# The last batch's feed-forward in layer 3: written out for two tiles in turn, over three engines

## The chip, the cores and the metric

The kernel runs on one core of one Trainium2 chip. The metric is the device time of one execution in microseconds (us). One further execution is recorded by the hardware profiler; its trace gives every instruction's start and duration, counted from the first instruction.

## What is computed

Four layers run one after the other on four batches of 256 tokens of 256 numbers. Each layer adds a cross-attention and a feed-forward to its input, each behind a layer norm. The change lies in the very last piece, layer 3's feed-forward, of which this is the core:

```python
def _quant_weight(w):
    scale = jnp.mean(jnp.abs(w)) + EPS
    wq = jnp.clip(jnp.round(w / scale), -1.0, 1.0)
    return (wq, scale)

def _quant_act(x):
    s = jnp.max(jnp.abs(x), axis=-1, keepdims=True) / 127.0 + EPS
    xq = jnp.clip(jnp.round(x / s), -128.0, 127.0)
    return (xq, s)

def _qlinear(x, w):
    wq, ws = _quant_weight(w)
    xq, xs = _quant_act(x)
    y = jnp.einsum('bsi,oi->bso', xq, wq)
    return y * xs * ws
gate = jax.nn.silu(_qlinear(x, w_gate))
up = _qlinear(x, w_up)
return _qlinear(gate * up, w_down)
```

Rows go in with 256 numbers, gate and up have 1024 columns, and down brings them back to 256. A row is rounded to whole numbers by its own largest magnitude, once ahead of gate and up and once more ahead of down.

## The kernel before

Tokens stand on the 128 partitions, so one batch is two tiles, q = 0 and 1. In layer 3 the attention of a batch is a long chain of score and value matmuls (`scores` and `values`), and the feed-forward of the batch before is put between them step by step: `ffn` is a Python generator, and each `yield` in it is a place where other work is written in between. For the last batch no attention is left. The end of `l3` (lines 2052 to 2066) closes the last head with `close`, forms the layer norm with `norms` and `normed`, and then steps the two generators of the two tiles in turn until both are done:

```python
            tail = [ffn(B - 1, q, xn, wide) for q in range(2)]
            while tail:
                tail = [t for t in tail if next(t, self) is not self]
```

Each engine carries out its instructions in the order in which they stand in its own queue, and waits at semaphores for the others. So this loop also sets the order in every queue: tile 0's step, tile 1's step, tile 0's next step. TensorE for instance gets gate of tile 0, gate of tile 1, up of tile 0, up of tile 1, for each half of 512 columns.

The steps of `ffn`, with their lines: `scale_of` takes the row maximum, the scale and its reciprocal (1859, 1860, 1862). Rounding is done by adding and subtracting a large constant RND: one operation scales and adds it (1869), the next subtracts it and clips above (1870), the third clips below and writes bf16 (1872). Two small products make the output scales `sg` (1874, 1875). The tile is transposed on TensorE (1879) and copied out of PSUM (1881). For each half of the 1024 columns follow two gate matmuls, silu as tanh on ScalarE (1890) with (1 + tanh) * gate on VectorE (1891), two up matmuls and the product of both (1896). Then the maximum over all 1024 columns (1859), the rounding in three operations of 1024 columns on VectorE (1900, 1902, 1904), eight transposes (1908), one copy (1910), eight down matmuls, the residual (1917) and the store by SP's DMA queue (1918). All elementwise work is VectorE's but the tanh. `close` ends a head: two transposes (1960), a division (1963, 1965) and two adds to the residual on GpSimd (1970). The statistics of the layer norm are at 1761 and 1762, the normalisation at 1767, the square root for it at 81. Matmuls are all issued by the helper `mm`, line 77. PSUM tiles of the tail come from the pool `ps_s`, three buffers of two banks each.

Of the kernel before, what the change touches and what calls it, by code (L numbers as in the profile page):

```python
# [11 lines left out]
F32 = mybir.dt.float32  # L12
BF16 = mybir.dt.bfloat16
# [4 lines left out]
AF = mybir.ActivationFunctionType  # L18
ALU = mybir.AluOpType
AX = mybir.AxisListType  # L20
# [3 lines left out]
P = 128  # L24
B = 4
S = 256
NT = B * S
D = 256
# [6 lines left out]
RND = 12582912.0  # L35
# [19 lines left out]
I3 = 1024  # L55
# [3 lines left out]
class Kernel:  # L59
# [1669 lines left out]
    def l3(self, first):  # L1729
# [9 lines left out]
        nc, tc, i = self.nc, self.tc, self.i  # L1739
        pairs = [tuple(range(m, min(m + 2, NM))) for m in range(0, NM, 2)]  # L1740
        with ExitStack() as es:
            one = es.enter_context(tc.tile_pool(name="a3one", bufs=1, reuse_waits="tile"))
            two = es.enter_context(tc.tile_pool(name="a3", bufs=2, reuse_waits="tile"))
            self.late3 = es.enter_context(tc.tile_pool(name="a3late", bufs=1, reuse_waits="tile"))
            ps_s = es.enter_context(tc.tile_pool(name="a3s", bufs=3, space=PSUM))
            ps = es.enter_context(tc.tile_pool(name="a3p", bufs=1, space=PSUM))
            ps_o = es.enter_context(tc.tile_pool(name="a3o", bufs=1, space=PSUM))
            mk, idb = self.mk3, self.idb
            self.va3.append(self.values3(self.late3))
            wq, ws = {}, {}  # L1750

            def bank():
                return ps.tile([P, 512], F32, name="b3", tag="tp")

            mv = one.tile([P, B, 2, 2], F32, name="mv3")
            rs = one.tile([P, B, 2], F32, name="rs3")

            def stats(b):
                for q in range(2):
                    t = self.small.tile([P, 6], F32, name="st3")  # L1760
                    nc.vector.bn_stats(t, self.x[b][:, q, :])
                    nc.vector.bn_aggr(mv[:, b, q, :], t)

            def normed(b, r):
                xn = self.xn.tile([P, 2, D], F32, name="xn3", tag="xn")
                for q in range(2):
                    nc.vector.tensor_scalar(
                        xn[:, q, :], self.x[b][:, q, :], mv[:, b, q, 0:1], r[:, q : q + 1], ALU.subtract, ALU.mult
                    )
                return xn  # L1770

            def norms(bs):

                for b in bs:
                    stats(b)
                v = slice(bs[0], bs[-1] + 1)
                self.rstd(rs[:, v, :], mv[:, v, :, 1], 1.0, self.eps5)
# [78 lines left out]
            def scale_of(v, name):  # L1856

                s = self.small.tile([P, 1], F32, name=name + "s")
                nc.vector.tensor_reduce(s, v, AX.X, ALU.max, apply_absolute_value=True)
                nc.vector.tensor_scalar(s, s, 1.0 / 127.0, 1e-5, ALU.mult, ALU.add)  # L1860
                r = self.small.tile([P, 1], F32, name=name + "r")
                nc.vector.reciprocal(r, s)
                return s, r

            def ffn(b, q, xn, take):

                v = xn[:, q, :]
                xs, r = scale_of(v, "xq3")
                nc.vector.tensor_scalar(v, v, r, RND, ALU.mult, ALU.add)
                nc.vector.tensor_scalar(v, v, RND, 127.0, ALU.subtract, ALU.min)  # L1870
                vb = two.tile([P, D], BF16, name="xb3")
                nc.vector.tensor_scalar(vb, v, -128.0, None, ALU.max)
                sg = self.small.tile([P, 3], F32, name="sg3")
                nc.vector.tensor_scalar(sg[:, 0:1], xs, ws["l3_wg"], 0.5, ALU.mult, ALU.mult)
                nc.vector.tensor_scalar(sg[:, 1:2], xs, ws["l3_wu"], sg[:, 0:1], ALU.mult, ALU.mult)
                yield
                tp = take(BF16)[:, : 2 * P].rearrange("p (k t) -> p k t", k=2)
                for k in range(2):
                    nc.tensor.transpose(tp[:, k, :], vb[:, k * P : (k + 1) * P], idb)
                xT = two.tile([P, 2, P], BF16, name="xqT3")  # L1880
                nc.vector.tensor_copy(xT, tp)
                yield
                g = two.tile([P, I3], F32, name="g3")
                for c in range(0, I3, 512):

                    pg = take(F32)
                    for k in range(2):
                        self.mm(pg, xT[:, k, :], wq["l3_wg"][:, k, c : c + 512], k == 0, k == 1)
                    gc = g[:, c : c + 512]
                    nc.scalar.activation(gc, pg, AF.Tanh, scale=sg[:, 0:1])  # L1890
                    nc.vector.scalar_tensor_tensor(gc, gc, 1.0, pg, ALU.add, ALU.mult)
                    yield
                    pu = take(F32)
                    for k in range(2):
                        self.mm(pu, xT[:, k, :], wq["l3_wu"][:, k, c : c + 512], k == 0, k == 1)
                    nc.vector.scalar_tensor_tensor(gc, pu, sg[:, 1:2], gc, ALU.mult, ALU.mult)
                    yield
                hs, r = scale_of(g, "hq3")
                yield
                nc.vector.tensor_scalar(g, g, r, RND, ALU.mult, ALU.add)  # L1900
                yield
                nc.vector.tensor_scalar(g, g, RND, 127.0, ALU.subtract, ALU.min)
                hb = two.tile([P, I3], BF16, name="hb3")
                nc.vector.tensor_scalar(hb, g, -128.0, None, ALU.max)
                yield
                tp = take(BF16).rearrange("p (k t) -> p k t", t=P)
                for k in range(I3 // P):
                    nc.tensor.transpose(tp[:, k, :], hb[:, k * P : (k + 1) * P], idb)
                hT = two.tile([P, I3 // P, P], BF16, name="hT3")
                nc.vector.tensor_copy(hT, tp)  # L1910
                yield
                o = take(F32)[:, :D]
                for k in range(I3 // P):
                    self.mm(o, hT[:, k, :], wq["l3_wd"][:, k, :], k == 0, k == I3 // P - 1)
                nc.vector.tensor_tensor(sg[:, 2:3], hs, ws["l3_wd"], ALU.mult)
                y = two.tile([P, D], F32, name="y3")
                nc.vector.scalar_tensor_tensor(y, o, sg[:, 2:3], self.x[b][:, q, :], ALU.mult, ALU.add)
                nc.sync.dma_start(self.out[b, q * P : (q + 1) * P, :], y)
# [35 lines left out]
                            m == 0, m == NM - 1,  # L1954
                        )

            def close(b, os, h, u):
                tp = bank().rearrange("p (q k) -> p q k", k=P)[:, :2, :]
                for q in range(2):
                    nc.tensor.transpose(tp[:, q, :], os[:, q * P : (q + 1) * P], self.ident)  # L1960
                tv = tp.rearrange("p q (r e) -> p q r e", e=32)
                rc = self.small.tile([P, 2, 4], F32, name="r3")
                nc.vector.reciprocal(rc, tv[:, :, :, HD3])
                t = two.tile([P, 2, 4, HD3], F32, name="t3")
                nc.vector.tensor_tensor(  # L1965
                    t, tv[:, :, :, :HD3], rc[:, :, :, None].to_broadcast([P, 2, 4, HD3]), ALU.mult
                )
                for q in range(2):
                    xt = self.x[b][:, q, h * P : (h + 1) * P].rearrange("p (r u d) -> p r u d", r=4, d=HD3)[:, :, u, :]
                    nc.gpsimd.tensor_tensor(xt, xt, t[:, q], ALU.add)  # L1970

            def beside(b, st):

# [50 lines left out]
            last = done = None  # L2024
            for b in range(B):
# [3 lines left out]
                for n, (h, u) in enumerate(heads):  # L2029
                    o = ps_o.tile([P, S], F32, name="o3")  # L2030
                    for c, ms in enumerate(pairs):
# [6 lines left out]
                        elif last is not None and last[5][-1] == NM - 1:  # L2038
                            os = two.tile([P, S], F32, name="os3")
# [5 lines left out]
                        last = (e, o, st["va"], h, u, ms, b)  # L2045
# [6 lines left out]
            values(*last[:6])  # L2052
            os = two.tile([P, S], F32, name="os3")
            nc.vector.tensor_copy(os, last[1])
            close(last[6], os, last[3], last[4])

            def wide(dt):
                return ps_s.tile([P, 1024 if dt is F32 else 2048], dt, name="w3", tag="s3")[
                    :, : 512 if dt is F32 else 1024
                ]  # L2060

            norms([B - 1])
            xn = normed(B - 1, rs[:, B - 1, :])
            tail = [ffn(B - 1, q, xn, wide) for q in range(2)]
            while tail:
                tail = [t for t in tail if next(t, self) is not self]

    def run(self):
        tc = self.tc
# [157 lines left out]
```

## Time and profile before

| | us |
|---|---|
| median of 8 runs | 2569.15 (2564.02 to 2572.76) |
| the profiled execution's own time | 2570.58 |
| its span, first to last instruction | 2568.8 |
| last attention matmul ends | 2540.25 |
| last VectorE instruction (residual of tile 1) ends | 2565.95 |
| TensorE busy in the whole span | 2435.7 (95%) |
| VectorE, ScalarE, GpSimd busy in the whole span | 1407.7, 1311.1, 841.6 |

In the profile PE is TensorE, DVE VectorE, ACT ScalarE, POOL GpSimd and SP the engine that issues DMAs. A row of a timeline gives start, duration, engine, line, operation, output and inputs, sizes and count; in square brackets stands how long the engine had been idle, and what ended that. Instructions of one line that follow each other are put into one row. A row of a group gives the total busy time and the mean duration in ns behind the bar. The granted clock is the share of its full clock that TensorE was allowed.

### The profile page before, as it was taken

The numbers are of one execution on the slowest core, as the hardware profiler recorded it, in microseconds if no ns is written. First come the engines' busy times: TensorE is split into PE (matmuls) and PEld (weight loads), VectorE is DVE, ScalarE is ACT, GpSimd is POOL, SyncE is SP. The second block draws the span as 40 slices with busy tenths as digits, with TensorE's granted clock in tenths as the row PEclk, the third lists the DMA queues.
The fourth block names the chain that finished last, engine by engine and source line by source line (L and its number), as shares of the span: only waits on it lengthen the run. The fifth ranks groups of instructions, "written<-read, shape, count | busy, mean of one in ns | idle before, by whom it ended". The sixth has DMA issues, their size and how long they took to land.

```text
span 2568.8 us, 47102 instructions
## 1 busy us (share of the span) xinstructions
PE 2435.7 (95%) x17623; PEld 1510.3 (59%) x17623; DVE 1407.7 (55%) x2915; ACT 1311.1 (51%) x3000; POOL 841.6 (33%) x1516
## 2 busy tenths in 40 slices
PE   8989987899989999999999999998999999999997
PEld 5778876777645555555555555565554544544553
DVE  5453534843567777777777777763324324334323
ACT  3234444533654545554545454423336766757875
POOL 1015645223345555555555555541011001011000
PEclk9999998989999999999999999998999999999998
DMA  7165675624601111111111111004310100000000
GB/s 251 49 212 156 175 148 156 215 88 138 224 19 48 47 48 48 47 47 48 47 48 48 47 48 47 9 1 176 125 56 28 34 2 28 6 1 2 6 6 5
DMA packets 96474, 188.45 MB, mean 73 GB/s; under 512 B 15401, under 2 KB 64297, under 8 KB 95050
## 3 DMA queue, kind: packets, MB, share of 16 engines
q1 hardware_dynamic: 80102, 146.50, 17.1%
q0 software_dynamic: 10416, 28.46, 4.8%
q10 hardware_dynamic: 5732, 10.49, 1.3%
q8 instruction: 143, 2.34, 0.4%
q14 instruction: 81, 0.66, 0.1%
HBM read 137.29 MB, written 48.11 MB: 72 GB/s over the span
## 4 chain that ended last, share of the span: by engine, by line
PE 84%; DVE 5%; ACT 3%; issue 3%; DMA 2%; POOL 1%; another core or an unknown queue 0%; ACTq 0%; PEld 0%; SPq 0%; POOLq 0%; DVEq 0%; PEldq 0%
PE s L77 25%; PE o L77 24%; PE fill L1241 3%; PE f2gu L77 3%; PE b L77 3%; PE f1gu L77 2%; PE acc L77 2%; PE tpq L77 2%; PE f0gu L77 2%; PE tpkv L77 2%; PE av L77 2%; PE f0y L77 2%; PE filly L1241 2%; PE f2y L77 1%; PE s L254 1%
## 5 line engine op out<-in xcount | busy, mean ns | idle before, releaser
L1487 ACT ACTIVATE p<-s,nmsm 128x448 f32<-128x448 f32 (+1 forms) x512 | 326.5, 644 | 381.2 <-PE s L77 247.2
L1943 ACT ACTIVATE e<-s 128x1024 f32<-128x1024 f32 (+1 forms) x448 | 404.3, 960 | 159.4 <-PE s L77 154.4
L77 PE MATMUL o<-pT,va 128*128 128x256 f32 (+2 forms) x1920 | 434.2, 379 | 9.5 <-DVE pT L1528 8.0
L77 PE MATMUL s<-kT,qT 128*32 128x448 f32 (+1 forms) x4096 | 427.4, 558 | 11.6 <-ACT kT L1459 8.2
L77 PEld LDWEIGHTS o<-pT,va 128*128 128x128 f32 (+1 forms) x1920 | 347.5, 192 | 130.5 <-issue 89.6
L1522 POOL TENSOR_SCALAR p<-p,rm 128x448 f32<-128x448 f32 (+1 forms) x512 | 324.5, 655 | 6.2
L1483 DVE TENSOR_REDUCE nmsm<-s 128x2 f32<-128x896 f32 (+1 forms) x256 | 287.5, 1124 | 7.9
L77 PE MATMUL s<-qb,kT 32*128 32x256 f32 (+1 forms) x3328 | 268.0, 405 | 11.0 <-ACT e L1943 11.0
L1528 DVE STREAM_TRANSPOSE pT<-p 128x896 f32<-128x896 f32 (+1 forms) x256 | 270.7, 1111 | 9.5 <-POOL p L1522 8.8
L77 PEld LDWEIGHTS s<-kT,qT 128*32 128x32 f32 x4096 | 120.2, 110 | 264.0 <-issue 239.0
L77 PE MATMUL o<-e,va 128*32 128x256 f32 (+1 forms) x3328 | 236.3, 392 | 1.2 <-DVE os L2040 1.2
L77 PEld LDWEIGHTS s<-qb,kT 32*128 32x128 f32 (+1 forms) x3328 | 163.3, 181 | 105.2 <-issue 75.5
L1515 POOL TENSOR_TENSOR rm<-em,tot 32x8 f32<-32x8 f32 x256 | 54.6, 213 | 400.0 <-DVE tot L1512 388.8
L1241 PE MATMUL fill<-wkc_early,ctxT 128*128 128x256 f32 (+1 forms) x572 | 148.7, 412 | 13.9 <-ACT kT_early L1277 12.1
L1970 POOL TENSOR_TENSOR x<-x,t 128x32 f32<-128x32 f32 x64 | 14.7, 252 | 439.6 <-DVE t L1965 439.6
L77 PEld LDWEIGHTS o<-e,va 128*32 128x32 f32 (+1 forms) x3328 | 90.6, 110 | 115.1 <-issue 74.9
L1480 DVE TENSOR_TENSOR s<-s,mask 128x128 f32<-128x128 f32 (+1 forms) x256 | 84.3, 330 | 104.6 <-PE s L77 92.4
L1241 PEld LDWEIGHTS fill<-wkc_early,ctxT 128*128 128x128 f32 (+1 forms) x572 | 114.9, 205 | 36.9 <-ACT kT_early L1277 14.5
L458 POOL DMA_INDIRECT f0xr<-f0xd,f0src x95 | 90.9, 957 | 69.5 <-PE f0y L77 24.4
L1487 ACT ACTIVATION_READ_ACCUMULATOR p<-s,nmsm 128x1 f32 x512 | 101.3, 198 | 0.0
L77 PE MATMUL f2gu<-f2wgu,f2xsT 128*128 x176 | 85.6, 611 | 0.6 <-ACT f2xsT L74 0.3
L566 POOL DMA_INDIRECT f0yt<-f0yd,f0slot x64 | 63.1, 986 | 60.2 <-DVE x L558 29.0
(488 smaller groups left out, 3510.6 us busy)
## 6 DMA issues: line engine op xcount, KB each, us to landing
ctxT<-in_ctxT SPq DMA_DIRECT2D x9, 1664.0 KB
vd<-va_early SPq DMA_DIRECT2D x96, 128.0 KB
kd<-kT_early SPq DMA_DIRECT2D x48, 256.0 KB
kT<-kd SPq DMA_DIRECT2D x16, 768.0 KB
va<-vd SPq DMA_DIRECT2D x16, 768.0 KB
f0yd<-f0ys SPq DMA_DIRECT2D x95, 128.0 KB
wq<-in_l_wq SPq DMA_DIRECT2D x16, 512.0 KB
wo<-in_l_wo SPq DMA_DIRECT2D x16, 512.0 KB
```

The costliest lines, as they stand in the source:

```text
L77: self.nc.tensor.matmul(out, lhsT, rhs, start=start, stop=stop, **kw)
L254: ins = nc.tensor.matmul(s[:, c0:c1], xT[:, k, q * P : (q + 1) * P], ctxT[b][:, k, c0:c1], start=k == 0, stop=k == 1)
L458: nc.gpsimd.indirect_dma_start(out=t, out_offset=None, in_=xd[:, :], in_offset=bass.IndirectOffsetOnAxis(ap=src[:, n : n + 1], axis=0),)
L566: nc.gpsimd.indirect_dma_start(out=yt, out_offset=None, in_=yd[:, :], in_offset=bass.IndirectOffsetOnAxis(ap=slot[:, t, r : r + 1], axis=0),)
L1241: ins = nc.tensor.matmul(tp[:rows, t, :], ctxT[u // NKV2][:, k, c0 : c0 + rows], w[u % NKV2][:, k, :], start=k == 0, stop=k == 1,)
L1480: nc.vector.tensor_tensor(sv, sv, mask[:, 2 * c : 2 * c + 2, : nt - CT, :].rearrange("p n t i -> p n (t i)"), ALU.add)
L1483: nc.vector.tensor_reduce(ms[:, 0, 2 * c : 2 * c + 2], s[:, :, : nt * 32], AX.X, ALU.max, negate=True)
L1487: nc.scalar.activation(p[:, n, : nt * 32], s[:, n, : nt * 32], AF.Exp, bias=ms[:, 0, e : e + 1], accum_out=ms[:, 1, e : e + 1],)
L1515: nc.gpsimd.tensor_tensor(r[32 * a : 32 * a + 32], e[:, a], tot, ALU.mult)
L1522: nc.gpsimd.tensor_scalar(p[:, n, : nt * 32], p[:, n, : nt * 32], r[:, e : e + 1], 1.0, ALU.mult, ALU.mult)
L1528: self.pin(nc.vector.transpose(pT[:, 2 * c : 2 * c + 2, :nt, :].rearrange("p n t i -> p n (t i)"), p[:, :, : nt * 32]))
L1943: nc.scalar.activation(e[:kr, :, :n, :], s[t][:kr, :, :n, :], AF.Exp, scale=1.0 / math.sqrt(HD3))
```

## The change

The last batch gets a method of its own, `last_tokens`, in place of the two generators. In the normalisation and the three roundings ahead of gate and up, tile 0 is VectorE's and tile 1 GpSimd's. The two tiles' first part is written first; then a loop does all the rest of tile 0 and then all the rest of tile 1. Gate and up of one half go to one PSUM tile of two banks. Silu is one ScalarE function that also scales, with its table loaded by an instruction of its own behind the square root. The row maximum is taken by halves into `mx` and then over those two. The first rounding operation ahead of down is a ScalarE activation (scale and RND as bias); the two clips stay with VectorE and go by halves, as do the transposes and copies, one copy on ScalarE and one on VectorE. The output scales are products on GpSimd. The second tile's store is issued by ScalarE. `close` gets a parameter, so that the last head's two adds run on VectorE.

```diff
-            def close(b, os, h, u):
+            def close(b, os, h, u, eng=nc.gpsimd):
...
-                    nc.gpsimd.tensor_tensor(xt, xt, t[:, q], ALU.add)
+                    eng.tensor_tensor(xt, xt, t[:, q], ALU.add)
...
-            close(last[6], os, last[3], last[4])
-
-            def wide(dt):
-                return ps_s.tile([P, 1024 if dt is F32 else 2048], dt, name="w3", tag="s3")[
-                    :, : 512 if dt is F32 else 1024
-                ]
-
-            norms([B - 1])
-            xn = normed(B - 1, rs[:, B - 1, :])
-            tail = [ffn(B - 1, q, xn, wide) for q in range(2)]
-            while tail:
-                tail = [t for t in tail if next(t, self) is not self]
+            close(last[6], os, last[3], last[4], nc.vector)
+
+            self.last_tokens(one, two, ps_s, mv, rs, stats, scale_of, wq, ws)
+
+    def last_tokens(self, one, two, ps_s, mv, rs, stats, scale_of, wq, ws):
...
+        nc, b, idb = self.nc, B - 1, self.idb
+        wide = lambda dt: ps_s.tile([P, 1024 if dt is F32 else 2048], dt, name="w3", tag="s3")
+        eng = (nc.vector, nc.gpsimd)
+        rnd = self.small.tile([P, 1], F32, name="rnd3")
+        nc.gpsimd.memset(rnd, RND)
+        stats(b)
+        self.rstd(rs[:, b, :], mv[:, b, :, 1], 1.0, self.eps5)
+
+        self.pin(nc.scalar.activation(self.small.tile([P, 1], F32, name="one3"), self.eps6, AF.Silu))
+        xn = self.xn.tile([P, 2, D], F32, name="xn3", tag="xn")
+        xT, sg = [], []
+        for q in range(2):
+            v = xn[:, q, :]
+            eng[q].tensor_scalar(
+                v, self.x[b][:, q, :], mv[:, b, q, 0:1], rs[:, b, q : q + 1], ALU.subtract, ALU.mult
+            )
+            xs, r = scale_of(v, "xq3")
+            eng[q].tensor_scalar(v, v, r, RND, ALU.mult, ALU.add)
+            eng[q].tensor_scalar(v, v, RND, 127.0, ALU.subtract, ALU.min)
+            vb = two.tile([P, D], BF16, name="xb3")
+            eng[q].tensor_scalar(vb, v, -128.0, None, ALU.max)
+            t = self.small.tile([P, 3], F32, name="sg3")
+            nc.gpsimd.tensor_tensor(t[:, 0:1], xs, ws["l3_wg"], ALU.mult)
+            nc.gpsimd.tensor_tensor(t[:, 1:2], xs, ws["l3_wu"], ALU.mult)
+            sg.append(t)
+            tp = wide(BF16)[:, : 2 * P].rearrange("p (k t) -> p k t", k=2)
+            for k in range(2):
+                nc.tensor.transpose(tp[:, k, :], vb[:, k * P : (k + 1) * P], idb)
+            t = two.tile([P, 2, P], BF16, name="xqT3")
+            nc.vector.tensor_copy(t, tp)
+            xT.append(t)
+        for q in range(2):
+            gq = two.tile([P, I3], F32, name="g3")
+            mx = self.small.tile([P, 2], F32, name="mx3")
+            for n, c in enumerate(range(0, I3, 512)):
+                w = wide(F32)
+                pg, pu = w[:, :512], w[:, 512:]
+                for t, name in ((pg, "l3_wg"), (pu, "l3_wu")):
+                    for k in range(2):
+                        self.mm(t, xT[q][:, k, :], wq[name][:, k, c : c + 512], k == 0, k == 1)
+                gc = gq[:, c : c + 512]
+                nc.scalar.activation(gc, pg, AF.Silu, scale=sg[q][:, 0:1])
+                nc.vector.scalar_tensor_tensor(gc, pu, sg[q][:, 1:2], gc, ALU.mult, ALU.mult)
+                nc.vector.tensor_reduce(mx[:, n : n + 1], gc, AX.X, ALU.max, apply_absolute_value=True)
+            s, r = scale_of(mx, "hq3")
+            hT = two.tile([P, I3 // P, P], BF16, name="hT3")
+            hb = two.tile([P, I3], BF16, name="hb3")
+            nc.gpsimd.tensor_tensor(sg[q][:, 2:3], s, ws["l3_wd"], ALU.mult)
+            for n, c in enumerate(range(0, I3, 512)):
+                gc, hc = gq[:, c : c + 512], hb[:, c : c + 512]
+                nc.scalar.activation(gc, gc, AF.Identity, bias=rnd, scale=r)
+                nc.vector.tensor_scalar(gc, gc, RND, 127.0, ALU.subtract, ALU.min)
+                nc.vector.tensor_scalar(hc, gc, -128.0, None, ALU.max)
+                tp = wide(BF16)[:, :512].rearrange("p (k t) -> p k t", t=P)
+                for k in range(4):
+                    nc.tensor.transpose(tp[:, k, :], hc[:, k * P : (k + 1) * P], idb)
+                (nc.vector.tensor_copy if n else nc.scalar.copy)(hT[:, 4 * n : 4 * n + 4, :], tp)
+            o = wide(F32)[:, :D]
+            for k in range(I3 // P):
+                self.mm(o, hT[:, k, :], wq["l3_wd"][:, k, :], k == 0, k == I3 // P - 1)
+            y = two.tile([P, D], F32, name="y3")
+            nc.vector.scalar_tensor_tensor(y, o, sg[q][:, 2:3], self.x[b][:, q, :], ALU.mult, ALU.add)
+            (nc.scalar if q else nc.sync).dma_start(self.out[b, q * P : (q + 1) * P, :], y)
```

## The prediction

> **What bounds the kernel now.** I read the page's first and fourth parts, then the timeline of the last 30 us by engine, then the granted clock by stage, and last the rows of operations that the change puts on another engine. The chain's shares by engine:
>
> ```profile
> PE 84%; DVE 5%; ACT 3%; issue 3%; DMA 2%; POOL 1%; another core or an unknown queue 0%; ACTq 0%; PEld 0%; SPq 0%; POOLq 0%; DVEq 0%; PEldq 0%
> ```
>
> TensorE bounds the kernel nearly everywhere, but not where the change lies. The last attention matmul ends at 2540.25 us; what follows is the last batch's feed-forward, 28.5 us up to 2568.8, and nothing of the next stage runs beside it. VectorE in that stretch (start, duration, operation, count):
>
> ```profile
> 2541.57 0.23 DVE L1965 TENSOR_TENSOR t<-b,r 128x64 f32<-128x64 f32 x1
> ...
> 2543.70 0.73 DVE L1767 TENSOR_SCALAR xn<-x,mv,rs 128x256 f32<-128x256 f32 x2
> 2544.35 0.74 DVE L1859 TENSOR_REDUCE xq3s<-xn 128x1 f32<-128x256 f32 x2
> ...
> 2547.26 0.29 DVE L1872 TENSOR_SCALAR xb<-xn 128x256 bf16<-128x256 f32 x1
> ...
> 2553.82 1.40 DVE L1896 SCALAR_TENSOR_TENSOR g<-w,sg,g 128x512 f32<-128x512 f32 x2
> 2555.14 2.33 DVE L1859 TENSOR_REDUCE hq3s<-g 128x1 f32<-128x1024 f32 x2
> ...
> 2557.78 1.40 DVE L1900 TENSOR_SCALAR g<-g,hq3r 128x1024 f32<-128x1024 f32 x2
> 2559.11 1.29 DVE L1902 TENSOR_SCALAR g<-g 128x1024 f32<-128x1024 f32 x2
> ...
> 2565.47 0.48 DVE L1917 SCALAR_TENSOR_TENSOR y<-w,sg,x 128x256 f32<-128x256 f32 x1 [0.39 <-PE w L77]
> ```
>
> The "x2" rows are the point: both tiles pass VectorE in turn, and it has no gap from 2550.47 to 2561.6. TensorE:
>
> ```profile
> 2547.61 0.40 PE L1879 MATMUL w<-idb,xb 128*128 128x128 bf16 x2 [0.65 <-DVE xb L1872]
> 2547.79 1.91 PE L77 MATMUL w<-l_wgb,xqT 128*128 128x512 bf16 x4
> 2549.50 1.56 PE L77 MATMUL w<-l_wub,xqT 128*128 128x512 bf16 x4
> 2561.05 1.89 PE L1908 MATMUL w<-idb,hb 128*128 128x128 bf16 x16 [7.16 <-DVE hb L1904]
> 2562.87 2.56 PE L77 MATMUL w<-l_wdb,hT 128*128 128x256 bf16 x16
> ```
>
> It idles 7 us in the middle. So VectorE bounds this stretch, with two tiles filling each other's waits. The granted clock in it (third figure from the right, after the five engines' busy times):
>
> ```profile
> 2543.90:2550.50 6.60, 3.29 (x11) 1.33 (x12) 4.66 (x22) 2.66 (x3) 0.00 (x0) 0.50 0.00 1
> 2550.60:2557.30 6.70, 2.83 (x10) 0.77 (x8) 6.62 (x9) 1.35 (x2) 0.00 (x0) 1.00 0.00 0
> 2557.50:2564.10 6.60, 3.05 (x22) 2.51 (x23) 5.55 (x14) 0.00 (x0) 0.00 (x0) 0.50 0.00 0
> ```
>
> After idling TensorE runs at 0.50; a 512-column matmul then takes 0.43 (eight from 2547.79 to 2551.21) instead of 0.3 (the four from 2551.21 in 1.25).
>
> **What decides: the order.** The changed program as built has, on TensorE: transposes of tile 0, transposes of tile 1, then gate, up, transposes and down of tile 0, and only then gate and up of tile 1. VectorE has the same order. So nothing of tile 1 past its transposes overlaps tile 0. The change takes VectorE's load away (four (1+tanh)*gate products of 0.69, two scalings of 0.70, half of the first roundings, four small scales), but it gives up the filling of one tile's waits by the other. I therefore add up a serial chain, twice.
>
> **Head.** The two residual adds move from GpSimd (0.25 each, first done at 2542.1, statistics from 2542.16) to VectorE; VectorE's nearest row is the 0.23 product of twice the size, and both adds now stand before the statistics: 0, within 0.1. Normalising tile 1 and its three roundings go to GpSimd, which shows no 128x256 of that operation. These are its bounds (ns of one behind the bar):
>
> ```profile
> L1522 POOL TENSOR_SCALAR p<-p,rm 128x448 f32<-128x448 f32 x256 | 160.0, 642 | 6.2
> L1515 POOL TENSOR_TENSOR rm<-em,tot 32x8 f32<-32x8 f32 x256 | 54.6, 213 | 400.0 <-DVE tot L1512 388.8
> L386 POOL TENSOR_SCALAR f0start<-tok 128x1 f32<-128x1 f32 x1 | 0.2, 243 | 0.0
> ```
>
> A straight line between 243 ns (1 column) and 642 (448) gives 0.47 for 256. VectorE saves one of its 0.37 normalisations, so tile 1's scale comes at about 2544.95 instead of 2545.27. In GpSimd's queue four one-column products stand ahead of the roundings: 4 x 0.21 = 0.84, to 2545.8; then 3 x 0.47 = 1.41, to 2547.2, against 2547.55 now. That is the lower end. The upper end comes from what VectorE's same instruction does beside GpSimd (minimum, median, maximum):
>
> ```profile
> L1767 DVE TENSOR_SCALAR xn<-x,mv,rs x12: 397/409/1335, 1925.4 to 2544.0; 128x256 f32<-128x256 f32 x12
> L1767 DVE TENSOR_SCALAR xn<-x,mv,ss x4: 694/1373/2050, 2153.2 to 2317.9; 128x256 f32<-128x256 f32 x4
> ```
>
> The second group runs while GpSimd normalises keys (2151.55 to 2158.32): it waits for whole GpSimd instructions. If every pair excludes the other, tile 1's first normalisation waits 0.37, and VectorE's three roundings of tile 0 (0.35 + 0.28 + 0.28) stand between GpSimd's: +1.28, to 2548.5. I take 2547.8, nearer the middle since the small products read little. [...] TensorE queues tile 0's gate behind tile 1's transposes, so everything waits for this. First gate matmul 0.24 later (as now, 2547.55 to 2547.79): **2548.05**, between 2547.45 and 2548.75; now 2547.79.
>
> **One tile, from its first gate matmul.** ScalarE's silu waits for gate and up of its half (the wait names the last up matmul): 4 x 0.43 + 0.24 until ScalarE begins (2548.65 to 2548.89 now) = 1.95. Silu 0.69 as the tanh: 2.64. Product with up 0.75 and a gap of 0.03: 3.42. Maximum of a half, 0.69 (the 128x512 row of L1724), to 4.14. The second product waits for that or for the second silu, 4.06 to 4.38, then 0.75 + 0.04 + 0.68: 5.6. Maximum of two, scale 0.15, reciprocal 0.16, gaps: 6.2. Rounding on ScalarE: 512 columns, 0.67 (0.65 for a square, 0.69 for a tanh): 6.9. Two clips of 512 columns on VectorE, 0.42 each (between 0.28 for 256 and 0.69 for 1024): 7.8. Four transposes at 0.107 + 0.22 (now 16 in 1.89): 8.45. ScalarE's copy of 512 columns 0.58: 9.1. Eight matmuls of 256 columns at 0.213: **10.8**, and 11.0 for y. The second half is ready by 9.6, when the first four matmuls still run. At the full clock this is 0.5 (four at 0.3), 0.2 (eight transposes took 0.62 at 2406.93) and 0.65 less (eight such matmuls took 1.05 at 2408.34): 9.45 and 9.65.
>
> **Sum.** Tile 0 at the low clock: 2548.05 + 10.8 = 2558.85 for tile 1's gate. Tile 1 between 9.65 and 11.0; I take 10.5, nearer the low clock, since TensorE again idles about 5 us in each tile: y starts at 2569.35, against 2565.47. That is **+3.9 us**; the end behind it stays (0.48 and 2.85 to the end of the span; the store now goes out by ScalarE's queue, where an issue takes 0.375 against 0.332, both rows of this trace). [...] The profiled execution took 2570.58, 1.4 above the median, so I put +3.85 on the median 2569.15: 2573.0.
>
> **Edits at no cost.** Silu's table load (1.28) follows the square root at 2543.5 and ends by 2544.8, five us before silu; today's tanh load ends at 2546.8, two us before its use, so nothing is gained either. If that cover went, 1.28 would show. The constant's memset (0.09) stands before GpSimd's mask conversion, which idles 66 us for a DMA. Both weight scales are done by 2545.8, needed at 2550; the third one (0.21) has 4 us. SP's queue only loses a store.
>
> **Rivals.** First, on the other side: GpSimd's chain ahead of tile 1's transposes is so slow that the kernel is slower beyond 0.2% (5.1 us, about what a measurement of this kernel can tell from no change). It decides from xb of tile 1 at 2549.05 on. For: the 1.3 to 2.05 us that VectorE's operation took beside GpSimd. Against: those GpSimd instructions were four times larger. With 0.9 instead of 0.47 for its four: +1.7, 2574.7. Chance 0.14. [...] Chance 0.18. Third: the change does overlap the tiles as its words say. VectorE then has 2 x 5.9 us (two products, two maxima, 0.44 small, four clips, copy, y) from 2550.7 on, and some 1 us of matmuls behind the last: y at 2563.5, -2, 2567. The built order speaks against it: 0.06, half of it beyond 0.2%. My forecast, +2.5 to +5.1, has 0.62. Range: +1.7 (all low ends) to +5.1 (2548.75 + 10.8 + 11.0 = 2570.55, all high ends), and up to +6.35 for the first rival; below, 0.85 us for the spread of the runs shown: 2570 to 2575.5. Slower 0.16 (the first rival and a rest of the forecast), faster 0.03, the same 0.81.
>
> **What would show it.** Right: tile 1's gate begins after tile 0's last down matmul, about 11 us after tile 0's; tile 1's xb on GpSimd ends between 2547.2 and 2548.5 on this clock; VectorE has gaps of us where it now has none; the granted clock is 0.50 in much of both tiles. Wrong: tile 1's matmuls between tile 0's, a tile under 9.5 us, GpSimd's 128x256 over 0.9, or a difference before 2541.5.

## The result and the profile after

The changed kernel takes 2577.08 us (median of 12 runs, 2572.39 to 2581.32), the kernel before beside it 2569.48 (34 runs). The ratio is 1.0030, 95% interval 1.0023 to 1.0038: some 7.7 us slower, where 3.85 were forecast and 2575.5 was the upper end of the range. The profiled execution took 2575.34, its span is 2573.6. Up to the last attention matmul both programs are the same, and in this execution the last head ends 3.6 us earlier than in that of before. All times below are therefore counted from one event, **the start of the copy of the last head's sums out of PSUM** (L2054; at 2540.30 before, 2536.71 after), and "the tail" is the stretch from there to the end of the span: 28.55 us before, 36.92 after, **+8.37**. Its three parts:

| us | before | after | difference | predicted |
|---|---|---|---|---|
| head: to the first gate matmul | 7.49 | 9.29 | +1.80 | +0.26 |
| tiles: from there to the start of the last residual (y) | 17.68 | 22.68 | +5.00 | +3.6 |
| end: from there to the end of the span | 3.38 | 4.95 | +1.57 | 0 |

The page's chain of waits moves by a hundredth (TensorE from 84% to 85%) and does not name the cause.

TensorE's timeline of the tail has the tiles one behind the other:

```profile
2545.81 0.39 PE L2090 MATMUL w<-idb,xb 128*128 128x128 bf16 x2 [1.98 <-POOL xb L2083]
2546.00 1.06 PE L77 MATMUL w<-l_wgb,xqT 128*128 128x512 bf16 x2
...
2554.25 0.61 PE L2118 MATMUL w<-idb,hb 128*128 128x128 bf16 x4 [4.63 <-DVE hb L2115]
...
2555.53 1.89 PE L77 MATMUL w<-l_wdb,hT 128*128 128x256 bf16 x8
2557.22 1.06 PE L77 MATMUL w<-l_wgb,xqT 128*128 128x512 bf16 x2
...
2566.70 1.89 PE L77 MATMUL w<-l_wdb,hT 128*128 128x256 bf16 x8
```

The first row waits for GpSimd's xb, and tile 0's gate stands right behind it. Tile 1's gate follows tile 0's last down matmul, 11.22 us after tile 0's. VectorE, which before ran from 2550.47 to 2561.6 without a gap, now waits by turns for ScalarE and TensorE:

```profile
2548.80 0.75 DVE L2105 SCALAR_TENSOR_TENSOR g<-w,sg,g 128x512 f32<-128x512 f32 x1 [2.26 <-ACT g L2104]
...
2553.30 0.43 DVE L2114 TENSOR_SCALAR g<-g 128x512 f32<-128x512 f32 x1 [0.88 <-ACT g L2113]
...
2557.52 0.48 DVE L2124 SCALAR_TENSOR_TENSOR y<-w,sg,x 128x256 f32<-128x256 f32 x1 [1.40 <-PE w L77]
...
2568.68 0.48 DVE L2124 SCALAR_TENSOR_TENSOR y<-w,sg,x 128x256 f32<-128x256 f32 x1 [1.40 <-PE w L77]
```

GpSimd's timeline shows the size that the head turned on (duration is the second figure), and a last small product at 2563.47:

```profile
2540.22 1.39 POOL L2076 TENSOR_SCALAR xn<-x,mv,rs 128x256 f32<-128x256 f32 x1 [13.64 <-DVE rs L82]
...
2543.07 0.58 POOL L2080 TENSOR_SCALAR xn<-xn,xq3r 128x256 f32<-128x256 f32 x1
2543.73 1.07 POOL L2081 TENSOR_SCALAR xn<-xn 128x256 f32<-128x256 f32 x1
2544.90 0.86 POOL L2083 TENSOR_SCALAR xb<-xn 128x256 bf16<-128x256 f32 x1
...
2563.47 0.19 POOL L2110 TENSOR_TENSOR sg<-hq3s,l_wds 128x1 f32<-128x1 f32 x1 [10.97 <-DVE hq3s L1860]
```

Four operations of one size took 1.39, 0.58, 1.07 and 0.86, where the forecast had 0.47 for each.

The granted clock in stretches of the tail (the third figure from the right; the figure behind the window's length is TensorE's busy time):

```profile
2546.20:2549.60 3.40, 3.40 (x9) 0.91 (x6) 1.06 (x3) 0.69 (x1) 0.00 (x0) 0.50 0.00 0
2550.40:2553.70 3.30, 0.00 (x0) 0.00 (x0) 2.28 (x6) 1.24 (x2) 0.19 (x1) 1.00 0.00 0
2553.90:2560.50 6.60, 6.06 (x24) 2.93 (x24) 2.51 (x6) 1.35 (x3) 0.00 (x0) 0.50 0.06 20
2560.70:2563.90 3.20, 0.08 (x1) 0.00 (x0) 2.60 (x6) 0.97 (x2) 0.19 (x1) 1.00 0.00 0
2564.10:2568.70 4.60, 2.99 (x16) 1.72 (x16) 2.06 (x6) 1.62 (x3) 0.00 (x0) 0.50 0.00 0
```

In the two tiles TensorE had the full clock only where it did almost nothing (1.00 with 0.00 and 0.08 us of work), and half of it (0.50) in nearly all its work. Last, the end of the program: the instructions of its closing line, L2223 before and L2282 after (engine's queue, operation, count: minimum, median and maximum in ns, first and last start). Before:

```profile
L2223 POOLq EVENT_SEMAPHORE  x4: 17/17/17, 2568.1 to 2568.7; - x4
L2223 POOLq DRAIN  x3: 45/107/9652, 2541.8 to 2568.6; - x3
L2223 SPq DRAIN  x3: 7/7/7, 2568.0 to 2568.3; - x3
```

After:

```profile
L2282 POOLq EVENT_SEMAPHORE  x4: 17/17/17, 2572.9 to 2573.5; - x4
L2282 POOLq DRAIN  x3: 45/107/9383, 2563.4 to 2573.4; - x3
L2282 SPq DRAIN  x3: 7/7/7, 2571.2 to 2573.1; - x3
```

GpSimd closes with a drain that lasts over 9 us in both. Before, GpSimd's last operation ended at 2542.33, its drain at 2551.49, in the shade of the feed-forward; the end came with SP's drain at 2568.0, when the last store had landed. After, the last operation ended at 2563.66 and the drain only at 2572.81, while SP's drain is done at 2571.3: GpSimd's semaphore event at 2572.9 opens the end.

So there were three theories for the parts, with rivals. **Head:** GpSimd's price, by the kind of operation or by VectorE's work beside it. **Tiles:** the serial order, at a low clock. **End:** GpSimd's closing drain behind the third scale product; the rival was that the last store is late because ScalarE issues it.

### The profile page after: what moved, and what is told of

Same layout as the page of the kernel before. It is cut to its first block, busy times and chain, and to the rows that moved or that the text cites. A ratio compares the mean times of both kernels' runs of the same rounds, so it can differ in the third digit from the quotient of the medians.

```text
span 2573.6 us, 47114 instructions
## 1 busy us (share of the span) xinstructions
PE 2437.2 (95%) x17623; PEld 1509.7 (59%) x17623; DVE 1402.5 (54%) x2909; ACT 1317.1 (51%) x3007; POOL 846.1 (33%) x1525
## 4 chain that ended last, share of the span: by engine, by line
PE 85%; DVE 5%; ACT 3%; DMA 2%; issue 2%; POOL 2%; another core or an unknown queue 1%; SPq 0%; ACTq 0%; PEld 0%; DVEq 0%; PEldq 0%; POOLq 0%
PE s L77 25%; PE o L77 24%; PE fill L1241 4%; PE f2gu L77 3%; PE b L77 3%; PE f1gu L77 2%; PE acc L77 2%; PE tpq L77 2%; PE f0gu L77 2%; PE filly L1241 2%; PE tpkv L77 2%; PE av L77 2%; DMA f0xr<-f0xd,f0src 2%; PE f2y L77 1%; PE f0y L77 1%
## 5 line engine op out<-in xcount | busy, mean ns | idle before, releaser
L1522 POOL TENSOR_SCALAR p<-p,rm 128x448 f32<-128x448 f32 (+1 forms) x512 | 324.4, 655 | 6.2
```

The source lines that it names most:

```text
L1522: nc.gpsimd.tensor_scalar(p[:, n, : nt * 32], p[:, n, : nt * 32], r[:, e : e + 1], 1.0, ALU.mult, ALU.mult)
```

## The experiments

Three chips served. The first four kernels ran beside a kernel before of 2568.8 us, experiments 5 to 8 on a chip where it takes 2526.5, and 9 and 10 on one where it takes 2525.8; so a time is compared only with its own neighbour. Tails are compared across: experiment 7, which leaves the tail as it is, has 28.55 us on its chip like the kernel before. Each time stands with the kernel before that shared its chip.

**1. The third scale product on VectorE.** Changed kernel, with

```diff
-            nc.gpsimd.tensor_tensor(sg[q][:, 2:3], s, ws["l3_wd"], ALU.mult)
+            nc.vector.tensor_tensor(sg[q][:, 2:3], s, ws["l3_wd"], ALU.mult)
```

> The tail is counted from the copy of the last head's sums out of PSUM (L2054) to the end of the span: 28.55 us in the kernel before, 36.92 in the changed one. Theory (a late GpSimd instruction keeps GpSimd's closing drain running after the last store): with the third scale on VectorE the last GpSimd work is tile 1's rounding, the barrier no longer waits for GpSimd, and 1.5 to 1.6 us go from behind the last y; tail 35.4. Rival (the store through ScalarE's queue costs it): nothing goes, 36.9.

Measured: 2574.70 against 2568.76, ratio 1.0026 (1.0014 to 1.0037); tail 35.33, which is 1.59 less, while y starts at 31.91 against 31.97. Its closing line:

```profile
L2282 POOLq EVENT_SEMAPHORE  x4: 17/17/17, 2570.2 to 2570.9; - x4
L2282 POOLq DRAIN  x3: 45/107/10058, 2543.8 to 2570.7; - x3
L2282 SPq DRAIN  x3: 7/7/7, 2570.1 to 2570.4; - x3
```

The drain now begins at 2543.8, GpSimd's event comes right behind SP's drain as it did before. From the start of y to the end it is 3.42 us, against 4.95 in the changed kernel and 3.38 before: the 1.57 of the end is GpSimd's, and the store, still issued by ScalarE here, has at most the 0.04 that is left.

**2. The second store issued by SP.** Changed kernel, with

```diff
-            (nc.scalar if q else nc.sync).dma_start(self.out[b, q * P : (q + 1) * P, :], y)
+            nc.sync.dma_start(self.out[b, q * P : (q + 1) * P, :], y)
```

> Only the last store moves back to SP's queue; the third scale stays on GpSimd. Theory (GpSimd's closing drain): tail unchanged, 36.9, within 0.2. Rival (the store through ScalarE's queue costs it): 35.4.

Measured: 2577.79, ratio 1.0032 (1.0021 to 1.0044); tail 36.91 against 36.92. The rival for the end falls: in the changed kernel it makes no difference which engine issues the store, since GpSimd's drain ends later (2579.0 in this run, where SP's first begins at 2577.4). What the store costs without that drain, experiment 1 shows.

**3. Tile 1's normalisation and roundings on VectorE.** Changed kernel, with

```diff
-        eng = (nc.vector, nc.gpsimd)
+        eng = (nc.vector, nc.vector)
```

> Normalisation and three roundings of tile 1 return to VectorE; all else as in the changed kernel. Theory (GpSimd's four 128x256 operations set the head, since tile 0's gate stands behind tile 1's transposes): the first gate matmul begins 7.0 to 7.4 us after L2054 instead of 9.3, and the whole 2 us are passed on: tail 34.9. Rival (the serial order of the tiles and the low clock are all of it, the head is covered): tail 36.5 or more.

Measured: 2574.86, ratio 1.0023 (1.0011 to 1.0035); tail 34.37, the first gate matmul at 7.10 instead of 9.29. TensorE's timeline:

```profile
2543.65 0.61 PE L2090 MATMUL w<-idb,xb 128*128 128x128 bf16 x4 [5.40 <-DVE xb L2083]
2544.43 1.04 PE L77 MATMUL w<-l_wgb,xqT 128*128 128x512 bf16 x2 [0.17 <-DVE xqT L2092]
```

One engine doing both tiles is 2.2 us earlier than two engines sharing them, and even 0.4 earlier than the kernel before. The tail gained 0.36 us more than the head: tile 1's last two up matmuls took 0.59 instead of 1.00, as at the granted clock of 1.00 in experiment 10.

**4. One late GpSimd instruction in the kernel before.** Two copies of a single column, one behind each tile's y; the rest is untouched and nothing reads them:

```diff
                     nc.vector.scalar_tensor_tensor(y, o, sg[:, 2:3], x, ALU.mult, ALU.add)
+                    if b == B - 1:
+                        nc.gpsimd.tensor_copy(self.small.tile([P, 1], F32, name="late"), y[:, 0:1])
```

> The kernel before with two more GpSimd instructions: each copies one column of a finished y tile to a place that nobody reads. Theory (about 9.2 us pass from GpSimd's last instruction to the end of its closing drain, and 0.8 more to the end): the last one ends about 26.2 us after L2054, so the tail is 36, 7 to 7.5 more than before, though the two together take 0.4 us and nobody waits for their data. Rival (the drain is short, or hidden behind the store): 28.6, no change.

Measured: 2577.87, ratio 1.0033 (1.0021 to 1.0045); tail 35.84 against 28.55, with y where it was. Its closing line:

```profile
L2225 POOLq EVENT_SEMAPHORE  x4: 17/17/17, 2572.8 to 2573.4; - x4
L2225 POOLq DRAIN  x3: 45/107/9360, 2563.4 to 2573.3; - x3
L2225 SPq DRAIN  x3: 7/7/7, 2565.4 to 2573.0; - x3
```

Two instructions of 0.19 and 0.18 us, placed late, cost the old kernel 7.3 us, nearly what the whole change costs. The drain again ended 9.16 us after the last of them. What the drain does in this time no trace shows.

**5. The changed kernel's operations, with the tiles in turn.** "In turn" means here a step of one tile, then a step of the other, as in the kernel before; the changed kernel runs the rest of the tiles one after the other. The loop over the rest becomes a generator, driven as the kernel before drives its own; engines and operations stay:

```diff
-        for q in range(2):
+        def rest(q):
...
                 nc.vector.tensor_reduce(mx[:, n : n + 1], gc, AX.X, ALU.max, apply_absolute_value=True)
+                yield
...
             nc.gpsimd.tensor_tensor(sg[q][:, 2:3], s, ws["l3_wd"], ALU.mult)
+            yield
...
                 (nc.vector.tensor_copy if n else nc.scalar.copy)(hT[:, 4 * n : 4 * n + 4, :], tp)
+                yield
...
+        tail = [rest(q) for q in range(2)]
+        while tail:
+            tail = [t for t in tail if next(t, self) is not self]
```

> The changed kernel with the rest of the two tiles written in turn, as the kernel before does it; every operation and its engine are the same. Theory (the order of the tiles is the largest part): VectorE gets both tiles' work without waits, about 10.1 us from its first product on; last y starts about 24.5 us after L2054 instead of 32.0, tail 28 to 28.5. Rival (the moved work and the clock cost it, in any order): tail 34 or more.

Measured: 2527.12 against 2526.53, ratio 1.0005 (0.9996 to 1.0015); tail 30.27. From first gate to last y it takes 17.57, against 22.68 in the serial order: **5.1 us are the order's**, as much as the whole difference of the tiles. The kernel before takes 17.68 for the same stretch, so the work that the change takes off VectorE gained only 0.1 here. GpSimd's last product ends at 18.91; with the 9.16 us of experiment 4 behind it, the drain is over by 28.07 (an estimate), 2.2 us ahead of the end: the earlier product hides the drain as well. The tail was expected 2 us shorter. The two tiles' sixteen down matmuls stand together at the granted clock of 0.50 (2518.0 to 2524.0) and take 3.62, which is 1.7 more than at the full clock in experiment 9; the rest of the miss stays open. The first gate matmul, these sixteen and the last y:

```profile
2506.87 0.63 PE L77 MATMUL w<-l_wgb,xqT 128*128 128x512 bf16 x1
...
2520.72 3.62 PE L77 MATMUL w<-l_wdb,hT 128*128 128x256 bf16 x16
...
2524.44 0.48 DVE L2127 SCALAR_TENSOR_TENSOR y<-w,sg,x 128x256 f32<-128x256 f32 x1 [1.22 <-PE w L77]
```

**6. TensorE kept busy, first try.** Changed kernel with filling matmuls of 512 columns whose result nobody reads: 30 ahead of the statistics, 12 behind gate and up of each tile.

```diff
+        def warm(n):
+            t = bank()
+            for _ in range(n):
+                self.pin(nc.tensor.matmul(t, self.idb, wq["l3_wg"][:, 0, :512], start=True, stop=True))
```

> The changed kernel with matmuls that nobody reads, to keep TensorE at work: 30 ahead of the first transposes, 12 behind gate and up of each tile. Theory (the low clock costs): granted clock 1.0 in both tiles, each tile 1.3 to 1.8 us shorter, tail 33 to 34. Rival (the low clock lies beside other waits, or the filling matmuls delay the real ones as much): tail within 1 us of 36.9.

Measured: 2533.84, ratio 1.0027 (1.0015 to 1.0039); tail 35.20, between what theory and rival expected. TensorE's filling ended too soon, and the clock still fell:

```profile
2508.90:2511.70 2.80, 2.75 (x13) 1.08 (x11) 2.48 (x4) 0.84 (x2) 0.00 (x0) 1.00 0.00 0
2511.70:2514.40 2.70, 0.03 (x1) 0.00 (x0) 1.68 (x7) 1.52 (x2) 0.19 (x1) 1.00 0.00 0
2514.40:2517.90 3.50, 3.10 (x18) 2.14 (x19) 1.14 (x3) 0.59 (x1) 0.00 (x0) 0.60 0.00 0
```

Twelve were busy for 2.75 us of a gap of 5.5. Then came 2.7 us without work and 0.4 us of transposes, and the clock was halved from 2515.1 to 2518.5 (worked out from the 0.60 of the last stretch and the 0.94 of the next one, 2517.9 to 2523.0). By itself this run does not settle what the clock is worth.

**7. GpSimd's operations alone.** Kernel before with 18 more operations of 128x256 on a scratch tile, each form three times, well ahead of the tail and read by nobody.

```diff
+                if b == B - 1:
...
+                    for _ in range(3):
+                        self.pin(nc.gpsimd.tensor_scalar(v, v, p0, p1, ALU.subtract, ALU.mult))
+                    yield
+                    for _ in range(3):
+                        self.pin(nc.gpsimd.tensor_scalar(v, v, p0, RND, ALU.mult, ALU.add))
+                    yield
...
```

The four other forms follow in the same way.

> The kernel before with 18 GpSimd operations of 128x256 on a tile that nobody reads, in the middle of the last batch's attention, three of each kind, where VectorE is mostly idle. Theory (the kind of operation sets the price): subtract and multiply about 1.1 us, multiply and add 0.58, subtract and minimum 1.07, maximum to bf16 0.86, as in the changed kernel. [...]

Measured: 2527.26 (one run), tail 28.55 as before. The groups, ns of one behind the bar, in the order subtract and multiply by two columns; add and minimum with constants; subtract and minimum; multiply by a column; maximum into bf16; multiply by a column and add a constant:

```profile
L2013 POOL TENSOR_SCALAR pv<-pv,mk 128x256 f32<-128x256 f32 x3 | 3.7, 1229 | 0.3
L2028 POOL TENSOR_SCALAR pv<-pv 128x256 f32<-128x256 f32 x3 | 3.2, 1072 | 0.3
L2019 POOL TENSOR_SCALAR pv<-pv 128x256 f32<-128x256 f32 x3 | 3.2, 1067 | 0.3
L2025 POOL TENSOR_SCALAR pv<-pv,mk 128x256 f32<-128x256 f32 x3 | 2.8, 924 | 0.3
L2022 POOL TENSOR_SCALAR pvb<-pv 128x256 bf16<-128x256 f32 x3 | 2.5, 848 | 0.2
L2016 POOL TENSOR_SCALAR pv<-pv,mk 128x256 f32<-128x256 f32 x3 | 1.4, 476 | 0.3
```

In the tail the four forms in use took 1.39, 0.58, 1.07 and 0.86; by themselves 1.23, 0.48, 1.07 and 0.85. So 3.62 of 3.90 us are **the kind of operation**, and 0.28 are left for VectorE's company or anything else that differs in the tail. Only multiply-and-add has the 0.47 of the forecast's straight line; a multiply alone takes 924 ns, twice as long.

**8. Undoing the three losses together:** edits 1, 3 and 5 in one kernel. What remains of the change is mainly silu as one function, maxima by halves and the rounding on ScalarE.

> Tiles in turn, the head on VectorE, the third scale on VectorE; silu as one function, maxima by halves and the rounding on ScalarE stay. Theory: first gate 7.1 us after L2054, last y at 22.3, tail 25.7, 2.9 us under the kernel before (0.11%). Rival (what the change takes from VectorE was not the bound): tail 28 to 29, the same as before.

Measured: 2523.88, ratio 0.9991 (0.9981 to 1.0001); tail 27.42, 1.1 below the kernel before, between what theory (25.7) and rival (28 to 29) expected. The interval holds 1, so the whole time does not tell this kernel from the one before. From first gate to last y it takes 16.91. The down matmuls are slow again:

```profile
2514.76 3.62 PE L77 MATMUL w<-l_wdb,hT 128*128 128x256 bf16 x16
```

**9. The same with TensorE filled,** by 22 matmuls ahead of the statistics and 26 behind both tiles' gate and up:

```diff
+        warm(22)
         stats(b)
...
+            if q:
+                warm(26)
```

> The kernel with tiles in turn and head and third scale on VectorE, with matmuls that nobody reads in TensorE's two gaps: 22 ahead of the first transposes, 26 behind the last up matmul. Theory (the low clock is what is left of the stretch): granted clock 1.0 up to the last down matmul, the 16 down matmuls 1.8 us instead of 3.6, first silu 0.9 us earlier; last y starts 21.5 to 22 us after L2054 instead of 24.0, tail 25 to 25.5, 0.13% under the kernel before. Rival (the filling matmuls hold up the real ones, or VectorE is the bound by now): tail 27 or more.

Measured: 2521.17 against 2525.83, ratio **0.9984 (0.9975 to 0.9993)**; tail 24.33. TensorE:

```profile
2506.02 5.78 PE L2060 MATMUL b<-l_wgb,idb 128*128 128x512 bf16 x25
...
2514.41 1.91 PE L77 MATMUL w<-l_wdb,hT 128*128 128x256 bf16 x16
```

The granted clock, third figure from the right:

```profile
2503.00:2512.00 9.00, 8.95 (x44) 3.93 (x42) 7.04 (x19) 4.74 (x7) 0.00 (x0) 1.00 0.00 0
2512.00:2516.00 4.00, 2.81 (x31) 2.13 (x29) 3.26 (x9) 1.88 (x4) 0.00 (x0) 1.00 0.00 0
```

Filling takes the place of the idle time, the granted clock is 1.0 up to the end of the last stretch read (2516.0, 20.6 us), and the same sixteen matmuls take 1.91 instead of 3.62. The tail is shorter than the 25 to 25.5 expected. This kernel is faster than both others: 4.2 us shorter in the tail than before, 12.6 shorter than the change.

**10. The changed kernel, with enough filling:** 36 matmuls ahead of the statistics, 23 behind gate and up of each tile.

> The changed kernel with 36 filling matmuls ahead of the first transposes and 23 behind gate and up of each tile, where 12 left 2.7 us of idling and a low clock behind them. Theory (the low clock costs about 2 us in each of the serial tiles): a tile takes 9.3 us from gate to gate instead of 11.2, last y starts 27.8 to 28.3 us after L2054 instead of 32.0; GpSimd's closing drain then ends last, about 10 us after the third scale of tile 1, so the tail is 33.4 to 34. Rival (the clock is a small part): last y at 30.2 as with 12, tail 35.

Measured: 2530.63 against 2525.83, ratio 1.0022 (1.0012 to 1.0031); tail 34.63. TensorE, the last y, and the granted clock in two stretches:

```profile
2503.71 0.60 PE L77 MATMUL w<-l_wgb,xqT 128*128 128x512 bf16 x2 [0.28 <-DVE xqT L2098]
...
2505.44 5.13 PE L2060 MATMUL b<-l_wgb,idb 128*128 128x512 bf16 x22
...
2511.95 1.25 PE L77 MATMUL w<-l_wdb,hT 128*128 128x256 bf16 x8
2513.04 0.59 PE L77 MATMUL w<-l_wgb,xqT 128*128 128x512 bf16 x2
```

```profile
2522.55 0.48 DVE L2131 SCALAR_TENSOR_TENSOR y<-w,sg,x 128x256 f32<-128x256 f32 x1 [0.76 <-PE w L77]
```

```profile
2504.00:2514.00 10.00, 9.21 (x51) 4.43 (x51) 5.78 (x13) 3.48 (x5) 0.19 (x1) 1.00 0.00 0
2514.00:2523.00 9.00, 7.74 (x43) 3.52 (x41) 5.74 (x13) 3.48 (x5) 0.19 (x1) 1.00 0.05 16
```

A tile from gate to gate takes 9.33 at the full clock and took 11.22. From first gate to last y it is 18.84 instead of 22.68: the clock is worth 3.84 us in the serial order. Order and clock are two losses, not one seen twice: with the tiles in turn the same stretch takes 16.91 with the sixteen down matmuls at 3.62 (experiment 8) and 13.93 at the full clock (experiment 9), so at the full clock the order is still worth 4.9 us. The first gate came at 9.99, later than the 9.29 without filling: 36 were a few too many, and these 0.7 us are what the tail lies above the expectation.

## Why the prediction was right and wrong

**Right: the order.** The serial chain of two tiles is what the instruction order showed and what ran; tile 1's gate follows tile 0's last down matmul. Experiment 5 puts 5.1 us on it. VectorE's gaps came as forecast, and so did the clock of 0.50. The rival of overlapping tiles falls for the changed kernel. A full clock through tile 1 had a chance of 0.18, and the range's lower end of +1.7 uses one; no run without filling matmuls shows it: in the changed kernel the granted clock was 0.50 in nearly all of both tiles' work.

**A term too small: the tile.** 10.8 was predicted for tile 0 from gate to gate, and 11.22 measured; 10.5 for tile 1 to its y, and 11.46 measured. Two steps failed in tile 1, by some half a microsecond each. One is the choice between the low and the high clock: "nearer the low clock" was still too near the high one, and the low clock's 11.0 lay nearer to the 11.46 than my 10.5. The other is the sum itself, which was short at the low clock too: it had 11.0 for y, and tile 0's y came after 11.52. Counted from tile 0's gate, ScalarE's rounding began at 6.46 where 6.2 stood, by small delays at the steps before, and the first clip at 7.30 where 6.9 stood, since the 512 columns took 0.84 us up to the first clip instead of some 0.7. At the full clock my sum was 9.45 for gate to gate; experiment 10 measured 9.33, so the list of steps was sound, though not each size: the gate and up matmuls taken at 0.3 each start 0.22 apart there, which made good what was short elsewhere.

**Wrong: "a straight line between 243 ns (1 column) and 642 (448) gives 0.47 for 256".** The row behind it (L1522, 642 ns for 448 columns) multiplies twice, which none of the four operations does, and the one behind the 243 ns (L386) multiplies once. Experiment 7 shows that on GpSimd the kind sets the price, from 476 to 1229 ns at one size. The mean of the four in the tail was 0.975, close to the 0.9 of the first rival, GpSimd's slow chain: for the head it had the mechanism right. Its +1.7 stood on top of the forecast's +0.26 for the head, nearly +2.0 together, against +1.80 measured. (The bound of +6.35 for this rival does not come out of the terms shown: 2548.05 + 1.7 + 10.8 + 11.0 gives +6.1.) The forecast's own signs of being wrong came: two of the four took over 0.9, and tile 1's xb ended at 2549.35 on the clock of before, where 2547.2 to 2548.5 was to be right. The head's upper bound was worked out from another cause, "if every pair excludes the other", and that is not what happened: VectorE's three roundings of tile 0 took 0.34, 0.30 and 0.30 us beside GpSimd, against 0.35, 0.29 and 0.29 before. VectorE's company was thus worth tenths here, 0.28 us at most in GpSimd's four operations (experiment 7), and the dear operation itself was what no bound held. Beside the keys, where the bound came from, GpSimd's instructions took 2.19 and 2.01 us; VectorE's two normalisations, 0.70 and 2.05, ended 0.15 us behind them (2153.89 and 2155.86 against 2153.74 and 2155.71).

**Wrong: "the end behind it stays", and "the third one (0.21) has 4 us".** The product indeed keeps nobody waiting who reads it. But it moves GpSimd's last instruction from 2.03 to 26.95 us into the tail, and the closing drain behind it ends 9.15 us later: +1.57. The trace of before had it (a drain of up to 9652 ns on POOLq at the closing line), but as a row of queue instructions that no busy view counts, and I did not ask what an engine still owes after its last operation. Experiments 1 and 4 show it by taking it away and by putting it alone into the kernel before.

The sum: 1.80 + 5.00 + 1.57 = 8.37 in place of 0.26 + 3.6 + 0. The head missed by 1.5, the tiles by 1.4, the end by 1.6; all three missed to the same side. Of the edits costed at nothing, silu's table and the memset do not stand in the chain of waits up to y, and the store by ScalarE costs 0.04 us at most (experiment 1). The first two scales do stand in that chain: tile 1's reciprocal was ready at 2542.45, and its rounding on GpSimd began at 2543.07, behind the products in GpSimd's queue. The head's sum had them, with 0.84 us.

## What to carry to other kernels

An order that runs two chains, independent of each other, one wholly behind the other pays each chain's waits in full: here 5.1 us, more than the 3.2 us of work that the change took off VectorE in the tail (busy 20.30 before, 17.12 after). So write the steps of both in turn and judge a change by the queue order before its instruction prices. Price a GpSimd operation only by a row of the same kind of operation (476 to 1229 ns at one size in experiment 7), and look at what an engine's last instruction has behind it until the program's end: a 0.19 us product cost 1.59 us here (experiment 1). In this tail, where TensorE waits for other engines, it did most of its work at a granted clock of 0.50; matmuls that nobody reads, in the gaps and no longer than them, gave 3.1 us back here (27.42 to 24.33).

## What was not expected of the hardware

- GpSimd's closing drain ended 9.16 us after its last operation in the kernel before, 9.15 in the changed one and 9.16 in experiment 4, whatever that operation was (an add of 32 columns, or a product or copy of one), and in the changed kernel the end of the program waits for it (drain over at 2572.81, GpSimd's semaphore event at 2572.86).
- GpSimd's operations with two steps at one size (128x256, float32) differ by 2.6 times: 476 ns for multiply and add, 1229 for subtract and multiply. A multiply alone took 924. Why, no run shows.
- In the two serial tiles the granted clock was 1.0 only in stretches where TensorE did almost nothing, and 0.50 in nearly all its work; in experiment 6 it fell after 2.7 us without work and 0.4 us with it. In the traces of both kernels the steps of the clock in the tail lie whole multiples of 3.41 us apart: at 3.44, 10.26, 17.09, 23.92 and 27.33 us behind L2054 before, and at 3.40, 13.64, 17.05, 23.88 and 27.29 in the changed kernel. In both of its tiles the full clock thus came when gate and up were done or nearly so.
